# A two-layer graph kernel: the first batch's scores computed from h transposed, with the small weight products placed after the second row of scores

## The chip, the cores and the metric

The kernel runs on one core of a Trainium2 chip. The metric is device time in microseconds (us) of one execution; times shown are medians of several executions.

The core's engines work side by side, each through its own queue in order: TensorE (PE; PEld is its weight load), VectorE (DVE), ScalarE (ACT), GpSimd (POOL) and SyncE (SP), which only issues transfers. Transfers are also issued by ScalarE and GpSimd. An instruction waits on semaphores until its inputs are written and its output's buffer is free, and everything behind it in its queue waits too. Matrix products go to PSUM; the kernel's other tiles lie in SBUF.

## What is computed

There are 16 batches of 1024 nodes with 128 features, and an adjacency matrix of 1024 x 1024 for each. Layer 0, cut to what matters here:

```python
h = jnp.einsum('bnf,df->bnd', x, Ww) + Wb
e = jnp.einsum('bjl,bkl->bjk', jnp.einsum('bjd,dl->bjl', h, A), h)
e = e + jnp.swapaxes(e, 1, 2)
scores = jnp.where(adj > 0, e, 0.0)
attention = jax.nn.softmax(scores, axis=1) * adj
h_prime = jax.nn.relu(jnp.einsum('bij,bjk->bik', attention, h))
```

Three gates follow, of the kind `sigmoid(h_prime @ wi_u + x @ wi_x)`, then a tanh, a residual sum and a layer norm. Layer 1 has four heads, each with scores, a tanh of adjacency times scores and a product with its own projection. Its heads are averaged, added to the input, and normalized again.

With S = A + A^T, the symmetric scores are e = h S h^T. Since h = x Ww^T + Wb, the same scores can be had from x directly: a matrix Q = Ww^T S Ww, a column c = Ww^T S Wb and a per-row constant replace h.

## The kernel before

**Tiling.** A batch's 1024 nodes are 8 blocks of 128. `R` (P x 8 x 8 x 128) holds the scores of one batch; `R[:, :, j, :]` is row block j. Since the scores are symmetric, `score(j)` computes only the blocks from the diagonal on (in halves of 512 columns), and `turn_score(j)` makes the mirrored blocks: in batch 0 by TensorE transposes and a ScalarE copy, later by VectorE and transfers. `find_edges(j)` (L391) makes the 0/1 mask from the adjacency, `mask(j)` (L401) multiplies it in and takes the row maximum on VectorE, then takes the exponential on ScalarE. `weigh(j)` (L414) takes the reciprocal of the sum, scales h's block into `hz`, multiplies the row by the adjacency, and `back(j - 1)` (L431) accumulates the block before it into `acc`.

**Scores of all batches before the change.** `project_q` (L306) computes q^T = Q^T x^T + c, `score` multiplies a block of q^T with x^T, and ScalarE adds the row constant while it copies the product out (L353). That constant is the last column of `h`, which `multiply_h` and `add_h` (L323, L333) compute with width G = 132: 128 columns of h, three columns of x's gate products, and this constant. Hence the first batch's score copies need `h`, and `h` needs `wwT_g` with its gate columns and `wb_row` with its last column.

**The weights.** The top of the kernel loads A, Ww and the small vectors, then forms `a_sym` = A + A^T, `wwT`, `s_ww` = S Ww, `q_w` = Q and `c_col`, one after the other (L139 to L153). `weigh_bias` (L155) adds the three gate columns and S Wb, `finish_weights` (L161) the last constant. Between them `keep_at_work` has TensorE multiply zeros. `join_weights` (L166) prepares layer 1's weights in four parts; its first part is a subtraction on GpSimd (L169).

**Order.** The order of work is written by hand (`manual_schedule`). `run(first, "...")` issues the named pieces of batch 0: Qn is `project_q`, Hn and hn are `multiply_h` and `add_h` for groups of three blocks, En `find_edges`, Sn `score`, Tn `turn_score`, An `mask`, Bn `weigh`; "S1.0" is one half of row 1. Every engine's queue follows that order. Before, batch 0's order is:

```python
run(first, "Q0")
weigh_bias()
run(first, "H0")
finish_weights()
run(first, "h0 E0 E1 S0 T0.0 S1.0 T0.1 S1.1 A0 E2 Q1 T1 S2 A1 E3 H1 h1 B0 T2 S3 A2 E4 B1")
```

From batch 0's end on, a loop over 16 x 32 steps runs layer 1 of one batch with layer 0 of the next.

**Buffers.** All products of this part come from one PSUM pool of four buffers (`small` and the scores, tag "sc"), handed out in turn: a product waits for whoever reads the one four before. Transfers issued from SP and ScalarE share eight semaphores, handed out in program order, and so a transfer waits for the eighth before it: the adjacency loads (L300) wait for the small loads ahead of them.

Of the kernel before, what the change touches and what calls it, by code (L numbers as in the profile page):

```python
# [19 lines left out]
P = 128  # L20
# [4 lines left out]
def two_layer_adjacency_kernel(  # L25
# [29 lines left out]
    sb = ctx.enter_context(tc.tile_pool(name="sb", bufs=2))  # L55
# [5 lines left out]
    def small(name):  # L61
        return ps_sc.tile([P, 512], F32, tag="sc", name=name)
# [4 lines left out]
    ident = consts.tile([P, P], F32, name="ident")  # L67
# [2 lines left out]
    nc.gpsimd.memset(mhalf, -0.5)  # L70

    a_in = sb.tile([P, P], F32, tag="hz", name="a_in", bufs=4)
    nc.scalar.dma_start(a_in, A)
    ww_in = sb.tile([P, P], F32, tag="hz", name="ww_in", bufs=4)
    nc.sync.dma_start(ww_in, Ww)
    wb_col = consts.tile([P, 1], F32, name="wb_col")
    nc.scalar.dma_start(wb_col, Wb.rearrange("(d o) -> d o", o=1))
    rows_x = sb.tile([3, P], F32, tag="s1", name="rows_x", bufs=4)
    for g, w in enumerate((wi_x, wf_x, wo_x)):
        nc.scalar.dma_start(rows_x[g : g + 1], w.rearrange("(o d) -> o d", o=1))  # L80


    G = D + 4
# [4 lines left out]
    wwT = wwT_g[:, :D]  # L88
# [46 lines left out]
    def keep_at_work(n):  # L135
        for _ in range(n):
            nc.tensor.matmul(idle[:, :P], warm[:, :P], warm[:, :P], start=True, stop=True)  # L137

    keep_at_work(6)  # L139
    pa, pw, ps, pc = small("p_a"), small("p_ww"), small("p_s"), small("p_c")  # L140
    nc.tensor.transpose(pa[:, :P], a_in, ident)
    nc.vector.tensor_add(a_sym, pa[:, :P], a_in)
    nc.tensor.matmul(pw[:, :P], ww_in, ident, start=True, stop=True)
    nc.scalar.copy(wwT, pw[:, :P])
    nc.gpsimd.tensor_copy(b_wide, wb_col.to_broadcast([P, P]))
    nc.tensor.matmul(ps[:, :P], a_sym, ww_in, start=True, stop=True)
    nc.vector.tensor_copy(s_ww, ps[:, :P])
    keep_at_work(1)
    pq, px = small("p_q"), small("p_x")
    nc.tensor.matmul(pq[:, :P], s_ww, ww_in, start=True, stop=True)  # L150
    nc.vector.tensor_copy(q_w, pq[:, :P])
    nc.tensor.matmul(pc[:, 0:1], s_ww, wb_col, start=True, stop=True)
    nc.vector.tensor_copy(c_col, pc[:, 0:1])  # L153

    def weigh_bias():  # L155
        nc.tensor.matmul(px[:, :3], rows_x, ident[:3, :3], start=True, stop=True)
        nc.vector.tensor_copy(gate_x, px[:, :3])
        nc.tensor.matmul(px[:, 3:4], a_sym, wb_col, start=True, stop=True)
        nc.vector.tensor_copy(sb_col, px[:, 3:4])

    def finish_weights():  # L161
        pt = small("p_bsb")
        nc.tensor.matmul(pt[:, :1], b_wide, sb_col, start=True, stop=True)
        nc.vector.tensor_copy(wb_row[:, G - 1 : G], pt[:, :1])
# [118 lines left out]
    def layer0(b):  # L283
# [5 lines left out]
        t = {}  # L289
# [16 lines left out]
        def project_q(q):  # L306
            if q == 0:
                t["qT"] = sb.tile([P, N], F32, tag="qT0", name=f"qT0_{b}", bufs=1)
            if (b, q) == (0, 1):
                ps = small("pT_q0_second")  # L310
                nc.tensor.matmul(ps, q_w, t["xT"][:, 512:], start=True, stop=True)
                nc.vector.tensor_scalar_add(t["qT"][:, 512:], ps, c_col)
                return
            if (b, q) != (0, 0):
                return project_T(t["qT"], q_w, t["xT"], c_col, f"q0_{b}", [q])
            ps = small("pT_q0_first")
            nc.tensor.matmul(ps, q_w, t["xT"][:, :512], start=True, stop=True)
            for at, to in ((0, P), (P, 512)):
                nc.scalar.activation(
                    t["qT"][:, at:to], ps[:, at:to], AF.Identity, bias=c_col  # L320
                )

        def multiply_h(g):  # L323

# [18 lines left out]
        def score(j, halves=None):  # L343
            if j == 0 and "R" not in t:

                t["R"] = sb.tile([P, NB, NB, P], F32, tag="R", name=f"R_{b}", bufs=1)
            for q in range(j // BH, NH) if halves is None else halves:
                ps = ps_sc.tile([P, 512], F32, tag="sc", name=f"sc0_{b}_{j}_{q}")
                lo, at = max(q * 512, j * P), (q + 1) * 512
                nc.tensor.matmul(  # L350
                    ps[:, : at - lo], t["qT"][:, ts(j, P)], t["xT"][:, lo:at], start=True, stop=True
                )
# [45 lines left out]
            engine.tensor_scalar(m, adj_t[b, j], 0.0, None, ALU.is_gt)  # L398
            t["edge", j] = m.rearrange("p (k d) -> p k d", d=P)

        def mask(j):  # L401
            s, nmax = t["R"][:, :, j, :], -3e38
            for ks in (ts(0, BH), ts(1, BH)) if (b, j) == (0, 0) else [slice(NB)]:
                top = sb.tile([P, 1], F32, tag="top", name=f"top_{b}_{j}_{ks.start}", bufs=4)
                nc.vector.tensor_tensor_reduce(  # L405
                    s[:, ks], s[:, ks], t["edge", j][:, ks], 1.0, nmax, ALU.mult, ALU.max, top
                )
                nmax = top
            nmax = sb.tile([P, 1], F32, tag="nmax", name=f"nmax_{b}_{j}", bufs=4)
            nc.vector.tensor_scalar_mul(nmax, top, -1.0)  # L410
            t["z", j] = sb.tile([P, 1], F32, tag="z", name=f"z_{b}_{j}", bufs=4)
            nc.scalar.activation(s, s, AF.Exp, bias=nmax, accum_out=t["z", j])  # L412

        def weigh(j):  # L414

            s = t["R"][:, :, j, :]
            adj = adj_t[b, j].rearrange("p (k d) -> p k d", d=P)
            rz = sb.tile([P, 1], F32, tag="rz", name=f"rz_{b}_{j}", bufs=4)
            t["hz", j] = sb.tile([P, D], F32, tag="hz", name=f"hz_{b}_{j}", bufs=4)
            nc.vector.reciprocal(rz, t["z", j])  # L420
            if b == 0 and j in (0, 1, NB - 3, NB - 2, NB - 1):
                nc.vector.tensor_scalar_mul(t["hz", j], t["h"][:, j, :D], rz)
            else:
                nc.scalar.mul(t["hz", j], t["h"][:, j, :D], rz)

            for ks in (ts(0, BH), ts(1, BH)) if (b, j) == (0, NB - 1) else [slice(NB)]:
                nc.vector.tensor_mul(s[:, ks], s[:, ks], adj[:, ks])  # L427
            if j:
                back(j - 1)
# [110 lines left out]
        def finish(p):  # L540
# [5 lines left out]
        pieces = {  # L546
            "W": load_xT, "X": load_x, "R": relu,
        }
# [15 lines left out]
        for q in range(NH):  # L564
            pieces[f"Q{q}"] = partial(project_q, q)
# [5 lines left out]
            if j + 1 < NB:  # L571
                pieces[f"T{j}"] = partial(turn_score, j)
        if b == 0:
            del pieces["S1"], pieces["T0"]
        if b == 1:
            del pieces["S0"]
            for q in range(NH):
                pieces[f"S0.{q}"] = partial(score, 0, [q])
        return pieces

    def run(pieces, names):
        for name in names.split():
            if name in pieces:
                pieces.pop(name)()
# [144 lines left out]
    first, second, join = layer0(0), layer0(1), join_weights()  # L729
# [2 lines left out]
    run(first, "X")  # L732
    run(second, "W")
    run(second, "L0 L1 L2 L3 L4 L5 L6 L7")
    run(first, "Q0")
    weigh_bias()
    run(first, "H0")
    finish_weights()
    run(first, "h0 E0 E1 S0 T0.0 S1.0 T0.1 S1.1 A0 E2 Q1 T1 S2 A1 E3 H1 h1 B0 T2 S3 A2 E4 B1")
    next(join)  # L740
    run(first, "H2 h2 T3 S4 A3 E5")
    next(join)
# [1 line left out]
    next(join)  # L744
    run(first, "B3 T5 S6 A5 E7")
    next(join, None)
    run(first, "B4 T6 S7 A6")
    run(second, "Q0")
    run(first, "B5 A7")
    run(second, "H0")  # L750
    run(first, "B6 B7 R")
    run(second, "h0 H1")
    run(first, "P")
    run(second, "h1")
# [131 lines left out]
```

## Time and profile before

| | |
|---|---|
| median of 3 runs | 2412.29 us (2412.1 to 2412.39) |
| profiled execution | 2412.01 us, of it a span of 2410.1 us |
| first scores start (TensorE) | 9.44 us |
| first half mask starts (VectorE) | 12.02 us |
| mask of row 1 starts | 15.48 us |
| mask of row 2 starts | 19.43 us |
| first product into `acc` | 19.56 us |
| last multiplication by adjacency ends | 41.1 us |
| batch 0's gates start (VectorE) | 46.43 us |

All entries below the second line are starts or ends in the profiled execution, counted from the span's start. In the views shown further on, a line gives start and length in us (or a group's busy time), the engine, the line of the program, the operation, output and inputs with their shape, and in brackets how long the engine had been idle and what ended that.

### The profile page before, as it was taken

How to read it: one execution, taken by the hardware profiler on the slowest of the kernel's cores; microseconds unless marked ns; L12 is line 12 of the kernel's file. 1: busy time of each engine (PE TensorE's matmuls, PEld its weight loads, DVE VectorE, ACT ScalarE, POOL GpSimd, SP SyncE). 2: the span in 40 equal slices, each digit the busy share in tenths (PEclk: the TensorE clock that was granted, in tenths of full speed). 3: DMA queues.
4: the chain of work that ended last, by engine and by line, in shares of the span. 5: the costliest groups of instructions: out<-in, count | busy, mean ns of one | idle time of the engine just before them, and what ended most of it. 6: DMA issues, size and time to landing. Idle time of an engine off the chain costs nothing.

```text
span 2410.1 us, 20163 instructions
## 1 busy us (share of the span) xinstructions
PE 2400.0 (100%) x5981; PEld 1095.2 (45%) x5981; DVE 1552.6 (64%) x3264; ACT 1062.2 (44%) x1499; POOL 609.1 (25%) x390
## 2 busy tenths in 40 slices
PE   9999999999999999999999999999999999999999
PEld 5444444444444444444444444444444444444444
DVE  7666666666667666676666665666666576666555
ACT  6544344444444444445344454434444344443333
POOL 1314131241312413123131231313214132141000
PEclk9999999999999999999999999999999999999999
DMA  5334151441514324143242422325233252341010
GB/s 186 79 76 126 37 139 35 95 115 48 127 44 100 101 54 122 51 108 86 61 114 58 114 73 70 105 61 122 62 77 107 52 127 57 80 114 34 18 27 10
DMA packets 474370, 197.05 MB, mean 82 GB/s; under 512 B 414980, under 2 KB 440323, under 8 KB 474260
## 3 DMA queue, kind: packets, MB, share of 16 engines
q1 hardware_dynamic: 455645, 129.03, 22.8%
q0 software_dynamic: 18320, 66.66, 9.3%
q8 instruction: 48, 0.79, 0.1%
q14 instruction: 63, 0.51, 0.1%
q10 hardware_dynamic: 294, 0.07, 0.0%
HBM read 136.19 MB, written 59.51 MB: 81 GB/s over the span
## 4 chain that ended last, share of the span: by engine, by line
PE 98%; DVE 2%; ACT 0%; issue 0%; POOLq 0%; DVEq 0%; ACTq 0%
PE sc L634 36%; PE acc L640 36%; PE acc L435 9%; PE sc L350 5%; PE pR L605 5%; PE pT_u L234 5%; PE pR_h L331 1%; PE pT_q L234 1%; DVE R L405 0%; DVE R L427 0%; PE idle L137 0%; DVE s L635 0%; DVE st L210 0%; DVE edge L398 0%; PE pt L454 0%
## 5 line engine op out<-in xcount | busy, mean ns | idle before, releaser
L635 DVE TENSOR_TENSOR s<-sc,adj 128x512 f32<-128x512 f32 x1008 | 685.2, 688 | 714.7 <-PE sc L634 693.5
L636 ACT ACTIVATE s<-s 128x1024 f32<-128x1024 f32 x504 | 533.0, 1058 | 1057.0 <-DVE s L635 893.5
L634 PE MATMUL sc<-uT,x1T 128*128 128x512 f32 x2048 | 962.7, 592 | 0.2
L640 PE MATMUL acc<-s,h 128*128 128x512 f32 x2016 | 947.3, 592 | 0.0
L640 PEld LDWEIGHTS acc<-s,h 128*128 128x128 f32 x2016 | 380.5, 190 | 484.7 <-issue 477.5
L634 PEld LDWEIGHTS sc<-uT,x1T 128*128 128x128 f32 x2048 | 386.7, 190 | 470.2 <-issue 403.2
L398 POOL TENSOR_SCALAR edge<-adj 128x1024 uint8<-128x1024 f32 x120 | 332.6, 2772 | 316.2 <-DVE top_None L405 313.8
L214 POOL TENSOR_TENSOR rs<-rs,mhalf 128x8 f32<-128x8 f32 (+3 forms) x35 | 54.1, 1546 | 884.1 <-DVE rs L213 884.1
L435 PE MATMUL acc<-R,hz 128*128 128x512 f32 x512 | 240.7, 593 | 1.3 <-DVE R L427 1.2
L412 ACT ACTIVATE R<-R,nmax 128x1024 f32<-128x1024 f32 x128 | 147.0, 1148 | 86.2 <-DVE nmax L410 77.4
L405 DVE CUSTOM_DVE_ANT_0 R<-R,edge 128x1024 f32<-128x1024 f32 (+1 forms) x128 | 154.8, 1209 | 0.6 <-PE turn L385 0.4
L427 DVE TENSOR_TENSOR R<-R,adj 128x1024 f32<-128x1024 f32 x129 | 154.5, 1198 | 0.0
L435 PEld LDWEIGHTS acc<-R,hz 128*128 128x128 f32 x512 | 96.7, 190 | 122.3 <-issue 115.2
L350 PE MATMUL sc<-xT,qT 128*128 128x512 f32 (+3 forms) x384 | 145.1, 487 | 0.6 <-ACT R L353 0.6
L353 ACT ACTIVATE R<-sc,h 128x512 f32<-128x512 f32 (+1 forms) x192 | 110.6, 579 | 51.4 <-PE sc L350 46.2
L467 POOL TENSOR_TENSOR x1T<-hp,wu_b 128x1024 f32<-128x1024 f32 x45 | 106.4, 2364 | 103.0 <-DVE hws L473 63.7
L234 PE MATMUL pT_u<-x1T,ms 128*128 128x512 f32 x256 | 120.6, 592 | 0.2 <-ACT x1T L598 0.2
L605 PE MATMUL pR<-cw,x1T 128*128 128x512 f32 x256 | 117.6, 598 | 0.0
L350 PEld LDWEIGHTS sc<-xT,qT 128*128 128x128 f32 x384 | 69.5, 190 | 71.0 <-issue 60.0
L300 POOL DMA_DIRECT2D adj<-in_adjT_dram x112 | 65.7, 587 | 92.5 <-DVE s L635 92.5
L658 DVE SCALAR_TENSOR_TENSOR sum<-acc,sum 128x512 f32<-128x512 f32 x95 | 61.3, 687 | 42.2 <-PE acc L640 42.2
L608 ACT COPY h<-pR 128x512 f32<-128x512 f32 x128 | 72.3, 592 | 28.3 <-PE pR L605 26.6
(144 smaller groups left out, 1131.5 us busy)
## 6 DMA issues: line engine op xcount, KB each, us to landing
adj<-in_adjT_dram POOLq DMA_DIRECT2D x112, 512.0 KB, 4.0
adj<-in_adjT_dram SPq DMA_DIRECT2D x16, 512.0 KB, 8.7
x<-in_x_dram SPq DMA_DIRECT2D x16, 512.0 KB, 5.6
xT<-in_xT_dram SPq DMA_DIRECT2D x15, 512.0 KB
dram_hp<-turn_hp SPq DMA_DIRECT2D x15, 512.0 KB, 2.6
hp<-dram_hp SPq DMA_DIRECT2D x60, 128.0 KB, 3.1
dram_x<-turn_x SPq DMA_DIRECT2D x15, 512.0 KB, 3.0
x1T<-dram_x SPq DMA_DIRECT2D x60, 128.0 KB, 5.8
```

The source lines that it names most:

```text
L234: nc.tensor.matmul(ps, w, src[:, ts(q, 512)], start=True, stop=True)
L350: nc.tensor.matmul(ps[:, : at - lo], t["qT"][:, ts(j, P)], t["xT"][:, lo:at], start=True, stop=True)
L398: engine.tensor_scalar(m, adj_t[b, j], 0.0, None, ALU.is_gt)
L405: nc.vector.tensor_tensor_reduce(s[:, ks], s[:, ks], t["edge", j][:, ks], 1.0, nmax, ALU.mult, ALU.max, top)
L412: nc.scalar.activation(s, s, AF.Exp, bias=nmax, accum_out=t["z", j])
L427: nc.vector.tensor_mul(s[:, ks], s[:, ks], adj[:, ks])
L435: nc.tensor.matmul(t["acc"][:, ts(q, 512)], t["hz", j], t["R"][:, ts(q, BH), j, :], start=(j == 0), stop=(j == NB - 1),)
L605: nc.tensor.matmul(ps, x1T_t[b][:, ts(k, P)], cw.rearrange("p h d -> p (h d)"), start=True, stop=True)
L634: nc.tensor.matmul(ps, x1T[:, ts(m, P)], uT[:, ts(q, 512)], start=True, stop=True)
L635: nc.vector.tensor_mul(s[:, ts(q, 512)], ps, adj[:, ts(q, 512)])
L636: nc.scalar.activation(s, s, AF.Tanh)
L640: nc.tensor.matmul(acc[:, ts(q, 512)], h1[:, ts(hd, D)], s[:, ts(q, 512)], start=(m == 0), stop=(m == NB - 1),)
```

## The change

Batch 0 takes its scores from h^T and g = S h^T. h^T is projected in two halves (`project_h`, `place_h`), g in three parts of 128, 384 and 512 columns (`project_g`; the first copied out by VectorE, the others by ScalarE), and the scores' copies are plain copies without a bias. Later batches keep Q, c and the row constant.

The weights' order follows: Ww and Wb's column are loaded first on ScalarE's queue, A third, the three row vectors on GpSimd's queue. The products for Q, c, the gate columns and S Wb (`weigh_all`) are issued after row 1's scores, and so are H0, `finish_weights` and h0. The first mask is split into halves issued apart from each other, with its exponential as a piece of its own. The edges of rows 1 to 4 move later in VectorE's queue. `hz` of blocks 1 and 5 is scaled by ScalarE instead of VectorE. At the end of batch 0, batch 1's Q0 and H0 move behind B5 and B6.

```diff
     a_in = sb.tile([P, P], F32, tag="hz", name="a_in", bufs=4)
-    nc.scalar.dma_start(a_in, A)
     ww_in = sb.tile([P, P], F32, tag="hz", name="ww_in", bufs=4)
-    nc.sync.dma_start(ww_in, Ww)
+    nc.scalar.dma_start(ww_in, Ww)
     wb_col = consts.tile([P, 1], F32, name="wb_col")
     nc.scalar.dma_start(wb_col, Wb.rearrange("(d o) -> d o", o=1))
+    nc.scalar.dma_start(a_in, A)
     rows_x = sb.tile([3, P], F32, tag="s1", name="rows_x", bufs=4)
     for g, w in enumerate((wi_x, wf_x, wo_x)):
-        nc.scalar.dma_start(rows_x[g : g + 1], w.rearrange("(o d) -> o d", o=1))
+        nc.gpsimd.dma_start(rows_x[g : g + 1], w.rearrange("(o d) -> o d", o=1))
...
     keep_at_work(6)
-    pa, pw, ps, pc = small("p_a"), small("p_ww"), small("p_s"), small("p_c")
-    nc.tensor.transpose(pa[:, :P], a_in, ident)
-    nc.vector.tensor_add(a_sym, pa[:, :P], a_in)
-    nc.tensor.matmul(pw[:, :P], ww_in, ident, start=True, stop=True)
+    pa, pw = small("p_a"), small("p_ww")
+    nc.tensor.transpose(pw[:, :P], ww_in, ident)
     nc.scalar.copy(wwT, pw[:, :P])
...
+    def sum_A():
+        nc.tensor.matmul(pa[:, :P], a_in, ident, start=True, stop=True)
+        nc.vector.tensor_add(a_sym, pa[:, :P], a_in)
+        nc.gpsimd.tensor_copy(b_wide, wb_col.to_broadcast([P, P]))
+
+    def weigh_Ww():
+        ps = small("p_s")
+        nc.tensor.matmul(ps[:, :P], a_sym, ww_in, start=True, stop=True)
+        nc.vector.tensor_copy(s_ww, ps[:, :P])
+
+    def weigh_all():
+        pq, px = small("p_q"), small("p_x")
+        nc.tensor.matmul(pq[:, :P], s_ww, ww_in, start=True, stop=True)
+        nc.tensor.matmul(px[:, 4:5], s_ww, wb_col, start=True, stop=True)
         nc.tensor.matmul(px[:, :3], rows_x, ident[:3, :3], start=True, stop=True)
+        nc.tensor.matmul(px[:, 3:4], a_sym, wb_col, start=True, stop=True)
+        nc.vector.tensor_copy(q_w, pq[:, :P])
+        nc.vector.tensor_copy(c_col, px[:, 4:5])
         nc.vector.tensor_copy(gate_x, px[:, :3])
-        nc.tensor.matmul(px[:, 3:4], a_sym, wb_col, start=True, stop=True)
         nc.vector.tensor_copy(sb_col, px[:, 3:4])
...
+        def project_h(q):
+
+            if q == 0:
+                t["hT"] = sb.tile([P, N], F32, tag="turn", name="hT", bufs=2)
+            hT, at = t["hT"], q * 512
+            ps = small(f"p_hT_{q}")
+            nc.tensor.matmul(ps, wwT, t["xT"][:, ts(q, 512)], start=True, stop=True)
+            if q:
+                t["p_hT"] = ps
                 return
...
             for at, to in ((0, P), (P, 512)):
-                nc.scalar.activation(
-                    t["qT"][:, at:to], ps[:, at:to], AF.Identity, bias=c_col
-                )
+                nc.scalar.activation(hT[:, at:to], ps[:, at:to], AF.Identity, bias=wb_col)
+
+        def place_h():
+            nc.vector.tensor_scalar_add(t["hT"][:, 512:], t["p_hT"], wb_col)
+
+        def project_g(at, to):
+            if at == 0:
+                t["qT"] = sb.tile([P, N], F32, tag="qT0", name=f"qT0_{b}", bufs=1)
+            ps = small(f"p_g_{at}")[:, : to - at]
+            nc.tensor.matmul(ps, a_sym, t["hT"][:, at:to], start=True, stop=True)
+            (nc.scalar.copy if at else nc.vector.tensor_copy)(t["qT"][:, at:to], ps)
...
                 nc.tensor.matmul(
-                    ps[:, : at - lo], t["qT"][:, ts(j, P)], t["xT"][:, lo:at], start=True, stop=True
+                    ps[:, : at - lo], t["qT"][:, ts(j, P)], t["xT" if b else "hT"][:, lo:at],
+                    start=True, stop=True,
                 )
+                if b == 0:
+                    nc.scalar.copy(
+                        t["R"][:, lo // P : at // P, j, :],
+                        ps[:, : at - lo].rearrange("p (k d) -> p k d", d=P),
+                    )
+                    continue
...
-            if b == 0 and j in (0, 1, NB - 3, NB - 2, NB - 1):
+            if b == 0 and j in (0, NB - 2, NB - 1):
                 nc.vector.tensor_scalar_mul(t["hz", j], t["h"][:, j, :D], rz)
             else:
                 nc.scalar.mul(t["hz", j], t["h"][:, j, :D], rz)
...
-    run(first, "Q0")
-    weigh_bias()
+    run(first, "K0")
+    sum_A()
+    run(first, "K1 g0 k1")
+    weigh_Ww()
+    run(first, "S0.0 S0.1 E0 T0.0 A0.0 g1 T0.1 A0.1")
+    run(first, "S1.0 S1.1 A0.e E1")
+    weigh_all()
     run(first, "H0")
     finish_weights()
-    run(first, "h0 E0 E1 S0 T0.0 S1.0 T0.1 S1.1 A0 E2 Q1 T1 S2 A1 E3 H1 h1 B0 T2 S3 A2 E4 B1")
+    run(first, "h0 T1 S2 A1 E2 g2 H1 h1 B0 E3 T2 S3 A2 E4 B1")
...
-    run(first, "B4 T6 S7 A6")
+    run(first, "B4 T6 S7 A6 B5 A7")
     run(second, "Q0")
-    run(first, "B5 A7")
+    run(first, "B6")
     run(second, "H0")
-    run(first, "B6 B7 R")
+    run(first, "B7 R")
```

Kn is `project_h`, k1 `place_h`, gn `project_g`, "A0.0" and "A0.1" the halves of the first mask and "A0.e" its exponential.

More of the change, by code (lines that the diff above doesn't have):

```diff
@@ L139, in two_layer_adjacency_kernel @@
     keep_at_work(6)
-    pa, pw, ps, pc = small("p_a"), small("p_ww"), small("p_s"), small("p_c")
-    nc.tensor.transpose(pa[:, :P], a_in, ident)
-    nc.vector.tensor_add(a_sym, pa[:, :P], a_in)
-    nc.tensor.matmul(pw[:, :P], ww_in, ident, start=True, stop=True)
+    pa, pw = small("p_a"), small("p_ww")
+    nc.tensor.transpose(pw[:, :P], ww_in, ident)
     nc.scalar.copy(wwT, pw[:, :P])
-    nc.gpsimd.tensor_copy(b_wide, wb_col.to_broadcast([P, P]))
-    nc.tensor.matmul(ps[:, :P], a_sym, ww_in, start=True, stop=True)
-    nc.vector.tensor_copy(s_ww, ps[:, :P])
     keep_at_work(1)
[L149 to L155, printed above, removed]
+    def sum_A():
[10 more added lines that the diff above has]
+        nc.tensor.matmul(px[:, 4:5], s_ww, wb_col, start=True, stop=True)
         nc.tensor.matmul(px[:, :3], rows_x, ident[:3, :3], start=True, stop=True)
+        nc.tensor.matmul(px[:, 3:4], a_sym, wb_col, start=True, stop=True)
+        nc.vector.tensor_copy(q_w, pq[:, :P])
+        nc.vector.tensor_copy(c_col, px[:, 4:5])
         nc.vector.tensor_copy(gate_x, px[:, :3])
-        nc.tensor.matmul(px[:, 3:4], a_sym, wb_col, start=True, stop=True)
         nc.vector.tensor_copy(sb_col, px[:, 3:4])
@@ L308, in project_q @@
                 t["qT"] = sb.tile([P, N], F32, tag="qT0", name=f"qT0_{b}", bufs=1)
[L309 to L312, printed above, removed]
+            project_T(t["qT"], q_w, t["xT"], c_col, f"q0_{b}", [q])
+        def project_h(q):
[6 more added lines that the diff above has]
+                t["p_hT"] = ps
                 return
[L314 to L317, printed above, removed]
             for at, to in ((0, P), (P, 512)):
-                nc.scalar.activation(
-                    t["qT"][:, at:to], ps[:, at:to], AF.Identity, bias=c_col
-                )
+                nc.scalar.activation(hT[:, at:to], ps[:, at:to], AF.Identity, bias=wb_col)
[7 more added lines that the diff above has]
+            (nc.scalar.copy if at else nc.vector.tensor_copy)(t["qT"][:, at:to], ps)
         def multiply_h(g):
@@ L399, in find_edges, with mask, exponentials @@
             t["edge", j] = m.rearrange("p (k d) -> p k d", d=P)
[L401 to L404, printed above, removed]
+        def mask(j, halves=None):
+            s, nmax = t["R"][:, :, j, :], t.get("top", -3e38)
+            for ks in [slice(NB)] if halves is None else [ts(q, BH) for q in halves]:
+                t["top"] = sb.tile([P, 1], F32, tag="top", name=f"top_{b}_{j}_{ks}", bufs=4)
                 nc.vector.tensor_tensor_reduce(
-                    s[:, ks], s[:, ks], t["edge", j][:, ks], 1.0, nmax, ALU.mult, ALU.max, top
+                    s[:, ks], s[:, ks], t["edge", j][:, ks], 1.0, nmax, ALU.mult, ALU.max, t["top"]
                 )
-                nmax = top
-            nmax = sb.tile([P, 1], F32, tag="nmax", name=f"nmax_{b}_{j}", bufs=4)
-            nc.vector.tensor_scalar_mul(nmax, top, -1.0)
+            if halves != [0]:
+                t["nmax", j] = sb.tile([P, 1], F32, tag="nmax", name=f"nmax_{b}_{j}", bufs=4)
+                nc.vector.tensor_scalar_mul(t["nmax", j], t.pop("top"), -1.0)
+            if halves is None:
+                exponentials(j)
+        def exponentials(j):
+            s = t["R"][:, :, j, :]
             t["z", j] = sb.tile([P, 1], F32, tag="z", name=f"z_{b}_{j}", bufs=4)
-            nc.scalar.activation(s, s, AF.Exp, bias=nmax, accum_out=t["z", j])
+            nc.scalar.activation(s, s, AF.Exp, bias=t["nmax", j], accum_out=t["z", j])
         def weigh(j):
@@ L573, in layer0 @@
         if b == 0:
-            del pieces["S1"], pieces["T0"]
-        if b == 1:
+            del pieces["S1"], pieces["T0"], pieces["A0"], pieces["Q0"], pieces["Q1"]
+            for q in range(NH):
+                pieces[f"K{q}"] = partial(project_h, q)
+                pieces[f"A0.{q}"] = partial(mask, 0, [q])
+            for g, (at, to) in enumerate(((0, P), (P, 512), (512, N))):
+                pieces[f"g{g}"] = partial(project_g, at, to)
+            pieces["k1"] = place_h
+            pieces["A0.e"] = partial(exponentials, 0)
+        if b <= 1:
             del pieces["S0"]
```

## The prediction

> **What bounds the kernel now.** I read the page first, then the chain of waits over the first 24 us, then the order of time there.
>
> ```profile
> span 2410.1 us, 20163 instructions
> PE 2400.0 (100%) x5981; PEld 1095.2 (45%) x5981; DVE 1552.6 (64%) x3264; ACT 1062.2 (44%) x1499; POOL 609.1 (25%) x390
> ```
>
> TensorE is busy 2400.0 of 2410.1 us, so no more than some ten microseconds can be won at all. The change touches only batch 0's first layer, the first 45 us. There the chain (start, length, what) is TensorE's until the first scores, then VectorE's:
>
> ```profile
> 8.68 0.78 PE pR_h L331 x6
> 9.47 0.12 PE p_bsb L163 x2
> 9.58 1.82 PE sc L350 x4
> ...
> 14.72 0.68 DVE qT L312
> ...
> 15.48 1.23 DVE R L405
> ...
> 17.50 0.48 DVE h L335
> ...
> 18.29 1.22 DVE R L427
> 19.51 1.14 DVE R L405
> ...
> 21.55 0.94 DVE hz L422
> ...
> 22.58 1.21 DVE R L427
> ```
>
> From 15.48 on VectorE runs mask (L405), edges, multiplication (L427) back to back, until 41.1. A shift of these steps moves all later work: at 57 us TensorE starts a stretch that hardly stops again. In order of time (start, length, engine, line) two more things are seen:
>
> ```profile
> 9.62 0.16 DVE L164 COPY wb_row<-p_bsb 128x1 f32<-128x1 f32 x1 [0.74 <-PE p_bsb L163]
> 9.81 0.57 DVE L335 TENSOR_TENSOR h<-pR_h,wb_row 128x396 f32<-128x396 f32 x1
> 20.90 1.68 POOL L169 TENSOR_TENSOR cw<-cw_in,cw_last 128x512 f32<-128x512 f32 x1 [0.41 <-DMA cw_in<-in_L_gnn_conv_w_dram]
> 21.55 1.11 DVE L422 TENSOR_SCALAR hz<-h,rz 128x128 f32<-128x128 f32 x1
> ```
>
> The small weight products and h's first add are over at 10.4, before any mask. And hz for block 1 takes 1.11 us where its kind takes 0.29: it ends as GpSimd's subtraction ends (22.58).
>
> **What the Trainium skill says.** "SBUF — State Buffer", Who interferes with whom: VectorE and GpSimd share a port pair, held for a whole instruction; a VectorE instruction in a two-port mode, or with two SBUF inputs beside a GpSimd read, is blocked. The 1.11 us agrees. "TensorE: Matmul & The Clock Gate", Part 1: TensorE starts at half clock and warms after some 3.4 us of work, at a varying moment. Agrees: weight loads take 337 ns until 5.5 us and 190 ns from 5.74. "DMA: Bandwidth & Descriptors", Queues, rings and completion order: an engine serves the queues in turn, so a small transfer waits behind packets of others. Wb's column (0.5 KB) took 3.8 us to land, Ww (64 KB) 2.1.
>
> **The change part by part.** Prices from the trace: a score of 512 columns holds TensorE 0.86 (two passes of 0.43), one of 384 0.65, a 128-column pass 0.11; a result reaches the next engine 0.3 after the last pass. I walk each engine's queue in the changed order, starting each step when its engine and inputs are free.
>
> 1. Front. Ww comes first on ScalarE's queue (issue 0.72, lands at 2.85 as before), and its transpose takes A's place at 3.76, so wwT is there at 4.4. h^T's first half is projected from 4.4; at half clock until 5.6 it takes 1.5 instead of 0.86, result 6.2. ScalarE's 128 columns: 6.65. A's transpose and sum lie behind: a_sym 6.8. h^T's second half 6.2 to 7.0, g's first block 7.0, VectorE's copy 7.5 to 7.8. First score at 7.84, was 9.44: 1.6 sooner. Unknown: Wb's column now feeds h^T; landing at 4.96 as before it has 1.2 us to spare, and A behind it must land by 5.95. How far the adjacency packets, now issued sooner, hold these two up no row shows. Bounds: nothing, or 0.5 late and then a_sym 0.5 late; a warm clock at 4.6 instead of 5.6 makes all 0.5 sooner. I take the old landings and the old clock.
> 2. First mask. Scores, turns and g1 (384 columns, put between the turns) give halves of the mask at 10.35 and 11.43, nmax at 12.3, was 13.89: lead 1.6. ScalarE's plain copies save 0.11 each (L353's 0.69 against L386's 0.58). Edge 0 sits ahead at 8.6; its adjacency landed at 9.45 before, but its issue no longer waits (2.96 was A's landing; now about 1.6), so about 8.1. Even at 9.45 it would be done before 10.35.
> 3. Small products. g1's copy is done at 11.5, so row 1's scores hold TensorE 11.5 to 13.1. Only then come p_q and three thin products (0.22 each): 13.1 to 14.0. VectorE has run out (edge 1 ends 13.0): q_w 13.6; its three copies from p_x start behind one wait, 14.24. Then pR_h needs gate_x: 14.5 to 15.26, p_bsb, wb_row 15.74, h's add 15.93, mask 1 at 16.4. It was 15.48. Lead of 1.6 has become a loss of 0.9. Row vectors moved to GpSimd's queue are wanted at 13.5 and wb_row's broadcast, now behind them, at 15.9; that broadcast landed 6.4 after its issue at 1.6, so about 2 us later still clears.
> 4. g's last part. Row 2's scores wait for the PSUM buffer that h's add frees: 16.53. Then S2.1, g2 (0.86, new in this place) until 18.76, H1, and h1's add at 19.7, was 17.42. VectorE idles 1.2 us. First multiplication 20.57, was 18.29: 2.3 late.
> 5. Edges. Edge 2, done ahead of mask 1 before, now lies behind it, and edge 3 behind the multiplication: 0.6 more. Mask 2 at 22.3, was 19.43: 2.9 late.
> 6. Weighting on ScalarE. Block 1's hz leaves VectorE: from its reciprocal to the multiplication 22.58 - 21.36 = 1.22 becomes 0.07, so 1.15 won. Block 5's: 0.39 becomes 0.07, 0.3 won. ScalarE has gaps of 0.7 to 1.5 before each exponential there, which hide 0.40 each; without them the accumulation, not the mask, would wait. 2.9 - 1.15 - 0.3 = 1.4 late.
> 7. GpSimd's subtraction. Its inputs are sooner by about what the adjacency gains, 1.3 or a little more, so it runs near 19 to 20.2. VectorE's gap of step 4 (18.5 to 19.7) covers it, and h1's add reads PSUM. From 0 (hidden) to 1.1 (half of 1024 columns' 2.36 is 1.2; all of it blocks if it starts under a mask); I take 0.3.
>
> Row sums (S0.0/S0.1 split, the later Q0 and H0 of batch 1) move nothing: TensorE waits for VectorE there. h^T uses a buffer of the transposes' pool, free again long before batch 1's first turn. Later batches have the same instructions in the same order.
>
> Sum: 1.4 + 0.3 = +1.7 us. The profiled execution took 2412.01 (span 2410.1 and 1.9 around it), 0.28 under the median 2412.29; against the median this gives 2414.0. My walk, done for the old order, met the old trace within 0.3 us at every mask, so 0.5 either way is its own error.
>
> **The rivals.**
> - Other side, faster: the lead survives. Mechanism: the small products really hide behind row 1's scores, so that mask 1 starts when its turns allow. S1.1 copied at 14.0, six turns 0.8: mask 1 at 14.7, h1 no later than before plus 0.4. Then +0.4 + 0.6 - 1.45 = -0.5, or with a warm clock -1.0: 2411.5. It decides if mask 1 starts before 15.0. For: TensorE has gaps there. Against: h's add stands ahead of mask 1 in VectorE's queue, and needs four hand-overs after 13.1.
> - Worse: the port clash falls on a mask (0.8 more) and Wb's column or A lands late behind adjacency packets (0.5 more): 2415.3. For: three adjacency loads now start with no wait. Against: the gap of step 4.
> - No difference: the two roughly cancel, within 0.3 us of 2412.3. It takes the walk to be off by 1.4.
>
> **How the numbers follow.** Forecast 0.58, worse 0.20, faster 0.13, none 0.09. Forecast's own range, +0.8 to +2.6, is walk error and the clash's ends. Leaving out part of the two outer cases: 2411.3 to 2415.6. A change of 0.2%, about what a measurement of this kernel can tell from no change, is 4.8 us. Every case lies inside it; 0.05 of the chances above goes to something unseen that carries a case beyond it (a change in the repeated part, or a row vector from GpSimd's queue that lands very late): faster 0.02, same 0.95, slower 0.03.
>
> **What would show it.** First score near 7.8 and nmax 0 near 12.3 (steps 1, 2); mask 1 after 16, with VectorE idle before wb_row (3); h1's add near 19.7, released by TensorE (4); mask 2 near 22 (5); hz of block 1 on ScalarE and mul 1 near 24.4 (6); GpSimd's subtraction near 19 (7). Mask 1 before 15.0, or h1's add before 18, would prove me wrong; so would any change of time between 100 and 2400 us.

## The result

| | before | after |
|---|---|---|
| median, 16 executions each | 2412.24 us (2411.88 to 2415.8) | 2417.72 us (2415.17 to 2419.08) |
| ratio, 95% interval | | 1.002 (1.0013 to 1.0027) |
| profiled execution | 2412.01 us | 2417.81 us |

The changed kernel is slower by 5.5 us. The forecast was +1.7 us; the measured time lies above its range and above the "worse" rival. The page of the changed kernel:

```profile
span 2415.9 us, 20184 instructions
PE 2403.4 (99%) x5987; PEld 1097.1 (45%) x5987; DVE 1552.1 (64%) x3263; ACT 1062.8 (44%) x1503; POOL 610.7 (25%) x393
```

TensorE's busy time rose by 3.4 us, the other engines' by less than 2, the span by 5.8. So TensorE stands idle 2.4 us longer and is slower over part of its work, and both have to be looked for in the first 52 us, where batch 0's first layer ends. The chain of waits of the changed kernel (start, length, what) begins with a line that the old one did not have:

```profile
1.64 7.35 DMA a_in<-in_L_gnn_A_dram
8.98 0.04 issue
9.03 0.80 PE p_a L146 x2
9.82 1.71 PE p_hT L322 x2
11.53 0.43 PE p_g L336 x2
11.96 0.39 PE p_s L152 x2
12.35 0.08 issue
12.43 1.95 PE sc L366 x4
...
21.00 1.23 DVE R L428
...
26.52 1.13 DVE R L428
```

A's transfer, third on ScalarE's queue, is issued at 1.64 and takes 7.35 us. The forecast needed it by 5.95; it came at 9.0. The first score starts at 12.43 instead of 7.84 (it was 9.44 before the change). In order of time (start, length, engine, line, operation; in brackets the idle time and what ended it):

```profile
9.03 0.80 PE L146 MATMUL p_a<-ident,a_in 128*128 128x128 f32 x2 [2.86 <-DMA a_in<-in_L_gnn_A_dram]
...
9.62 1.91 PE L322 MATMUL p_hT<-xT,wwT_g 128*128 128x512 f32 x2
```

TensorE stood idle for 2.86 us, and then the second half of h^T took 1.91. The table by stretches of time shows why (its first line names the columns: the stretch, its length, the busy time and instructions of each engine, the granted TensorE clock, the DMA engines' share, GB/s):

```profile
core 0: us, PE busy (x) PEld busy (x) DVE busy (x) ACT busy (x) POOL busy (x), PEclk, DMA share, GB/s
6.00:7.00 1.00, 0.17 (x1) 0.00 (x0) 0.00 (x0) 0.79 (x2) 0.00 (x0) 1.00 0.91 355
7.00:8.00 1.00, 0.00 (x0) 0.00 (x0) 0.00 (x0) 0.05 (x1) 0.00 (x0) 1.00 1.48 395
8.00:9.00 1.00, 0.00 (x0) 0.00 (x0) 0.00 (x0) 0.00 (x0) 0.00 (x0) 0.89 0.77 204
9.00:10.00 1.00, 0.97 (x3) 0.93 (x4) 0.14 (x1) 0.00 (x0) 0.00 (x0) 0.50 0.97 324
```

While TensorE waits, the DMA engines move 355 and 395 GB/s, far more than the 64 KB of A. And the granted clock, 1.00 at 6, is 0.50 at 9. Stretches of half a microsecond give 0.78 for 8.5 to 9.0 and 0.81 for 12.0 to 12.5, which puts the half clock at about 8.8 to 12.2. (A reading of 1.00 in this column does not prove full clock: in the run "column as one row" below, the first half of h^T took 2.08 us at readings of 1.00. The reading of 0.50 is trusted here because the duration of the products goes with it.)

From the first score on, the changed kernel runs almost as the forecast walked it. The table gives times after the start of the first score; "loads of before" is the experiment further down in which A is on time.

| after the first score, us | forecast | after | loads of before |
|---|---|---|---|
| first score itself starts at | 7.84 | 12.43 | 7.41 |
| mask of row 1 | 8.6 | 8.57 | 8.57 |
| h1's add | 11.9 | 11.41 | 11.32 |
| mask of row 2 | 14.5 | 14.01 | 14.04 |
| second multiplication | 16.6 | 16.01 | 16.93 |

Batch 0's gates start on VectorE at 51.97 (46.43 before): 5.54 late, the whole loss.

```profile
51.97 0.18 DVE L529 TENSOR_TENSOR gate<-hp,gate 128x24 f32<-128x24 f32 x1 [1.90 <-ACT hp L483]
```

The first score is 2.99 later than in the kernel before, and 4.59 later than the forecast had it (12.43 against 7.84), because the lead of 1.6 is gone too. So the first question is what held A, and the second whether the rest of the sum would have come true with A on time.

### The profile page after: what moved, and what is told of

Same layout as the page of the kernel before. It is cut to its first block, busy times and chain, and to the rows that moved or that the text cites. A ratio compares the mean times of both kernels' runs of the same rounds, so it can differ in the third digit from the quotient of the medians.

```text
span 2415.9 us, 20184 instructions
## 1 busy us (share of the span) xinstructions
PE 2403.4 (99%) x5987; PEld 1097.1 (45%) x5987; DVE 1552.1 (64%) x3263; ACT 1062.8 (44%) x1503; POOL 610.7 (25%) x393
## 4 chain that ended last, share of the span: by engine, by line
PE 97%; DVE 1%; DMA 1%; issue 0%; ACT 0%; SPq 0%; POOL 0%; ACTq 0%; POOLq 0%; DVEq 0%
PE sc L669 36%; PE acc L675 36%; PE acc L463 9%; PE sc L366 5%; PE pT_u L239 4%; PE pR L640 4%; PE pR_h L347 1%; PE pT_q L239 1%; DMA a_in<-in_L_gnn_A_dram 0%; DVE R L428 0%; DVE st L215 0%; DMA R<-dram_turn 0%; SPq L269 0%; DVE x L230 0%; DVE R L455 0%
## 5 line engine op out<-in xcount | busy, mean ns | idle before, releaser
L366 PE MATMUL sc<-xT,qT 128*128 128x512 f32 (+2 forms) x360 | 135.7, 487 | 0.6 <-ACT R L376 0.6
L376 ACT ACTIVATE R<-sc,h 128x512 f32<-128x512 f32 (+2 forms) x180 | 103.8, 579 | 48.3 <-PE sc L366 43.2
```

The source lines that it names most:

```text
L366: nc.tensor.matmul(ps[:, : at - lo], t["qT"][:, ts(j, P)], t["xT" if b else "hT"][:, lo:at], start=True, stop=True,)
```

## The experiments

Each kernel was run beside the kernel before on the same chip. "Gates" is the start of batch 0's gates on VectorE in the profiled execution, against 46.43 before.

| kernel | A lands | column lands | first score | gates later by | time against before, us | ratio, 95% interval |
|---|---|---|---|---|---|---|
| after | 9.0 | 5.7 | 12.43 | 5.54 | +5.5 | 1.0013 to 1.0027 |
| A before the column | 4.7 | 8.0 | 9.53 | 2.81 | +3.0 | 1.0005 to 1.0018 |
| row vectors on ScalarE | 9.4 | 5.3 | 12.94 | 7.01 | +6.0 | 1.0013 to 1.0027 |
| TensorE kept at work | 9.0 | 5.6 | 10.98 | 4.04 | +4.4 | 1.0007 to 1.002 |
| column as one row | 8.4 | - | 11.87 | 5.21 | +5.2 | 1.0012 to 1.0026 |
| adjacency held | 4.9 | 4.6 | 8.77 | 2.88 | +2.8 (one execution) | - |
| A first on SP | 2.7 | 5.3 | 8.06 | 2.43 | +2.3 | 1.0 to 1.0017 |
| loads of before | in time | 4.5 | 7.41 | 1.42 | +1.7 | 0.9997 to 1.0013 |
| products sooner | in time | 4.8 | 8.07 | -0.52 | 0.0 | 0.9991 to 1.0007 |
| subtraction on TensorE | in time | 5.0 | 9.30 | 2.03 | +1.4 | 0.9992 to 1.0008 |
| hz 1 and 5 on ScalarE alone | as before | as before | as before | -0.79 | -0.65 | 0.9988 to 1.0005 |

Landings are the issue time plus the transfer's time to landing. The columns of the gates and of the time agree within about 1 us in every row, so the stretch up to the gates does decide the time. Where an interval includes 1, the time alone does not tell the kernel from the one before, and only the traces speak. Each trace is one execution. The last row is the kernel before with one edit, "products sooner" and "subtraction on TensorE" build on "loads of before", and the other rows are the changed kernel with one edit.

**A before the column.** Is it A's size or its place?

```diff
     nc.scalar.dma_start(ww_in, Ww)
+    nc.scalar.dma_start(a_in, A)
...
     nc.scalar.dma_start(wb_col, ...)
-    nc.scalar.dma_start(a_in, A)
```

> The changed kernel with one edit: on ScalarE's queue A is issued ahead of Wb's column instead of behind it. Theory (A waits behind the column's 128 four-byte packets and the adjacency packets): A lands before 5 us instead of 9.0, TensorE doesn't stop at 6.2 and its clock doesn't fall back to half, first score near 7.8 to 8.5 instead of 12.4, time 2413.2 to 2414.2, that is +1.0 to +2.0 over before: what the forecast's walk had. Rival (adjacency traffic alone holds A, wherever it stands in its queue): A still lands after 8, time stays within 1 of 2417.7. Second rival (the time is lost in the later order, steps 3 to 5): A lands early and the time stays above 2416.

A, now second, took 3.5 us to land. The column, now third, with 0.5 KB, took 6.4 and held h^T, so that the first score and the time came later than expected (9.53, and 3.0 above the kernel before). So the place decides, or the moment of issue: in these two runs 1.2 was early enough and 1.6 was not. Size does not.

**Row vectors on ScalarE.** They go behind A as before the change. Through the eight shared semaphores, this makes all adjacency loads but the first wait for earlier loads again.

```diff
-        nc.gpsimd.dma_start(rows_x[g : g + 1], ...)
+        nc.scalar.dma_start(rows_x[g : g + 1], ...)
```

> The changed kernel with one edit: the three row vectors go back to ScalarE's queue, behind A, so that seven of the eight adjacency loads wait for small loads again, as before. Theory that early adjacency traffic holds A: A lands near 6, time 2414 to 2415. Rival that A's place behind Wb's column alone holds it: A still lands near 9, time within 1 of 2417.7.

A landed 7.8 us after its issue all the same. This seemed to clear the adjacency, but one line of the adjacency's transfers in that run, up to 1.9 us, says otherwise:

```profile
L305 SPq DMA_DIRECT2D adj<-in_adjT_dram x1: 432/432/432, 1.6 to 1.6; - x1
```

One load of 512 KB was still issued at 1.6, beside A, and three more at 3.7, 5.2 and 5.6, before A had landed. So this run left the cause open between these loads and the place in the queue. It lost more than the changed kernel, 7.0 us at the gates, and two things in its trace have a part in that: the half clock was granted from 8.06 to about 14.9, 6.8 us instead of 3.4, although TensorE worked again from 9.5 on, and mask 1 ran beside GpSimd's subtraction and took 2.14 instead of 1.23.

**TensorE kept at work.** Thirteen products of zeros fill the wait for A. How much of the loss is the clock?

```diff
     run(first, "K0")
+    keep_at_work(13)
     sum_A()
```

> The changed kernel plus 13 products of zeros on TensorE between h^T's first half and A's product, 2.8 us of work where it stood still. A still lands near 9. If the half clock from 8.9 to 12.2 us was a cost of its own: first score about 1 us sooner (11.4 instead of 12.4), time about 2416.7. If it cost nothing: within 0.3 of the changed kernel's own 2417.7.

A still landed at 9.0, but the second half of h^T took 1.02 instead of 1.91 and the first score started 1.45 us sooner:

```profile
9.35 1.02 PE L322 MATMUL p_hT<-xT,wwT_g 128*128 128x512 f32 x2
```

The half clock is worth 1.5 us at the gates (5.54 - 4.04). In the time it is 1.1 (5.5 - 4.4), a difference that the intervals alone would not show. The rest of A's lateness, against the forecast's first score, is 10.98 - 7.84 = 3.14.

**Adjacency held.** The adjacency loads are not issued until A is there.

```diff
         def load_adj(j):
...
+            if (b, j) == (0, 0):
+                nc.gpsimd.tensor_copy(a[:, :1], a_in[:, :1])
             (nc.sync if b < 2 else nc.gpsimd).dma_start(a, adjT[b, ts(j, P), :])
```

> The changed kernel, but the adjacency loads are not issued until A has landed: a GpSimd copy of one column of A into the first adjacency tile goes ahead of them. Theory 1 (adjacency packets, issued sooner than before, hold A up): A lands at 4.5 to 6. Theory 2 (its third place on ScalarE's queue, behind the column, holds it up, together with x^T's half-megabyte at most): A lands at 7.5 or later all the same. First adjacency row then lands 4 to 6 us after A, so the first edges and all later masks are later than in the changed kernel under theory 2.

The two answers of the trace for A's transfer, first of the changed kernel, then of this one. The second line of each gives the time from issue to landing:

```profile
L77 ACTq DMA_DIRECT2D a_in<-in_L_gnn_A_dram x1: 453/453/453, 1.6 to 1.6; - x1
...
DMA to landing us min/median/max: 7.3/7.3/7.3
```

```profile
L77 ACTq DMA_DIRECT2D a_in<-in_L_gnn_A_dram x1: 454/454/454, 1.6 to 1.6; - x1
...
DMA to landing us min/median/max: 3.2/3.2/3.2
```

Same queue, same place behind the column, same moment of issue: 7.3 against 3.2. The adjacency loads held A, for 4.1 us. What is ahead of A, the column and x^T, can account for no more than part of the 3.2. The row vectors gained too (2.5 to 3.5 us to landing instead of 6.3 to 7.3). Keeping the adjacency back cost nothing at the first edge, which ran at 9.39 without waiting for it. The first score, 8.77, would have come sooner still with the clock of the other runs: h^T's first half took 2.08 here and 1.40 in the changed kernel. This is one execution, but the 7.3 stands in two traces, of the changed kernel and of the one kept at work.

**Column as one row.** It comes as 512 bytes that TensorE turns, instead of 128 pieces of 4 bytes.

```diff
-    nc.scalar.dma_start(wb_col, Wb.rearrange("(d o) -> d o", o=1))
+    wb_in = sb.tile([1, P], F32, tag="s1", name="wb_in", bufs=4)
+    nc.scalar.dma_start(wb_in, Wb.rearrange("(o d) -> o d", o=1))
...
+    nc.tensor.matmul(pw[:, P : P + 1], wb_in, ident[:1, :1], start=True, stop=True)
+    nc.vector.tensor_copy(wb_col, pw[:, P : P + 1])
```

> The changed kernel, but Wb's column comes as one row of 512 bytes that TensorE turns, instead of 128 pieces of 4 bytes. Theory 2a (the column's 128 small packets hold A up): A lands at 4.5 to 5.5, the first score at 7.8 to 8.5, time 1.5 to 2.5 us above the kernel before. Theory 2b (third place holds it up whatever is ahead) or theory 1 (adjacency): A lands at 8 or later, first score after 11.5, time 4 us or more above.

A took 6.7 us, landing at 8.4, so the column's small packets account for about 0.6 of its 7.3 us. The packets in this trace show how A was held: between 3.6 and 5.5 us ScalarE's queue moved 0.06 MB in 126 packets, nearly all of A; the last few packets, 18 at most, took until 8.4, while SP's queue moved 0.84 MB between 5.5 and 8.5. The load counts as landed with its last packet.

**A first on SP.**

```diff
-    nc.scalar.dma_start(a_in, A)
+    nc.sync.dma_start(a_in, A)
```

> The changed kernel with one transfer moved: A goes first on SP's queue, ahead of x^T and the adjacency, and no longer third on ScalarE's. Theory (A was late because adjacency packets were issued ahead of it or beside it): A lands at 2.8 to 3.5, the column at 5 to 6, the first score at 7.8 to 8.8, mask 1 at 16.3 to 17.4, time 1.5 to 2.8 us above the kernel before. Rival (the column, too, is held up by the sooner adjacency and takes A's place as the last to land): column after 7, first score after 9.5, time 3 or more above.

```profile
L77 SPq DMA_DIRECT2D a_in<-in_L_gnn_A_dram x1: 382/382/382, 0.7 to 0.7; - x1
...
DMA to landing us min/median/max: 2.0/2.0/2.0
```

A landed 2.0 us after its issue, the column 4.1 after its own. One moved transfer takes 3.1 of the gates' 5.5 us away, while the adjacency is still issued right behind x^T, at 2.1 instead of 1.6.

**Loads of before.** The changed order of work, with the small loads on the queues and in the order that they had.

> The changed order of work, but all small loads as before: A first and Wb's column second on ScalarE's queue, the row vectors behind them, Ww first on SP. Theory (late A is what the forecast missed; its other steps hold): A lands near 2.9, the column near 5.0, TensorE does not idle and keeps its clock; first score 7.8 to 8.2, mask 1 16.2 to 16.8, h1's add 19.4 to 20.1, mask 2 22.0 to 22.7; time 1.2 to 2.2 us above the kernel before. Rival a (the later steps were mis-sized too and cost more than walked): 3 us or more above. Rival b (with the loads right the lead survives): no more than 0.3 above.

The median is 1.7 us above that of the kernel before (2413.92 against 2412.21). The interval still includes no change, so the trace has to carry this reading: the gates are 1.42 late. In order of time, the steps that the forecast named, with GpSimd's subtraction:

```profile
15.98 1.23 DVE L428 CUSTOM_DVE_ANT_0 R<-R,edge 128x1024 f32<-128x1024 f32 x1
...
18.73 0.57 DVE L351 TENSOR_TENSOR h<-pR_h,wb_row 128x396 f32<-128x396 f32 x1 [0.73 <-PE pR_h L347]
...
21.45 1.21 DVE L428 CUSTOM_DVE_ANT_0 R<-R,edge 128x1024 f32<-128x1024 f32 x1
...
22.77 1.57 DVE L421 TENSOR_SCALAR edge<-adj 128x1024 bf16<-128x1024 f32 x1
```

```profile
21.50 2.30 POOL L174 TENSOR_TENSOR cw<-cw_in,cw_last 128x512 f32<-128x512 f32 x1 [0.51 <-DMA cw_in<-in_L_gnn_conv_w_dram]
```

Mask 1 comes 15.98 - 15.48 = 0.5 later than in the kernel before although the first score is 2.0 sooner: the lead is lost in the small products, as step 3 said. An edge that takes 0.68 elsewhere takes 1.57 and ends at 24.34, after the subtraction's end at 23.80. The subtraction was blocked in its turn: it began at 21.50, beside the mask that ran from 21.45 to 22.66, and ended 1.14 after that mask.

**hz of blocks 1 and 5 on ScalarE alone**, in the kernel before.

```diff
-            if b == 0 and j in (0, 1, NB - 3, NB - 2, NB - 1):
+            if b == 0 and j in (0, NB - 2, NB - 1):
```

> The kernel before with one edit: hz of blocks 1 and 5 is scaled by ScalarE (step 6 alone). Forecast's working: VectorE saves 1.15 + 0.3, so 1.0 to 1.5 faster than before, 2410.8 to 2411.3, unless GpSimd's subtraction then blocks another VectorE instruction (edge 4 or the next mask) by up to 1.1; then 0 to 0.4 faster. Rival: the accumulation waits for ScalarE instead and nothing is won (within 0.2 of 2412.2).

The median is 0.65 us lower, with an interval that includes no change, and between the two amounts that the expectation had named; in the trace the gates come 0.79 sooner. The second multiplication started 1.2 sooner, at 21.39; but then GpSimd's subtraction met the next mask, which took 1.95 instead of 1.21:

```profile
22.14 1.58 POOL L169 TENSOR_TENSOR cw<-cw_in,cw_last 128x512 f32<-128x512 f32 x1 [0.28 <-DMA cw_in<-in_L_gnn_conv_w_dram]
```

```profile
22.86 1.95 DVE L405 CUSTOM_DVE_ANT_0 R<-R,edge 128x1024 f32<-128x1024 f32 x1
```

**Products sooner.** On top of the loads of before, the order that the steps 3 to 5 charge is mended.

```diff
     run(first, "S0.0 S0.1 E0 T0.0 A0.0 g1 T0.1 A0.1")
-    run(first, "S1.0 S1.1 A0.e E1")
     weigh_all()
-    run(first, "H0")
+    run(first, "S1.0 S1.1 A0.e E1 E2 H0")
     finish_weights()
-    run(first, "h0 T1 S2 A1 E2 g2 H1 h1 B0 E3 T2 S3 A2 E4 B1")
+    run(first, "h0 T1 S2 A1 E3 H1 h1 g2 B0 T2 S3 A2 E4 B1")
```

> As the version with all loads of before, and further: the small weight products are issued ahead of row 1's scores instead of behind them, edge 2 ahead of h's first add, edge 3 ahead of h's second, and g's last part behind H1. Theory (steps 3 to 5 of the forecast are losses of the order and not of the formula): mask 1 at 15.0 to 15.7, h1's add at 17.5 to 18.2, mask 2 at 19.5 to 20.3; time 0.2 to 1.5 us below the kernel before. Rival (small products now delay row 1's scores and turns by as much as they gain): mask 1 after 16, time 0.5 to 1.5 above the kernel before.

```profile
15.70 1.23 DVE L428 CUSTOM_DVE_ANT_0 R<-R,edge 128x1024 f32<-128x1024 f32 x1
...
19.64 1.22 DVE L428 CUSTOM_DVE_ANT_0 R<-R,edge 128x1024 f32<-128x1024 f32 x1
...
23.11 1.95 DVE L428 CUSTOM_DVE_ANT_0 R<-R,edge 128x1024 f32<-128x1024 f32 x1
```

The masks came as expected, the gain in time did not: the time is that of the kernel before (2412.2 against 2412.21), the gates are 0.5 sooner in the trace. Counted from the first score (8.07), mask 1 starts at 7.63 instead of 8.57, mask 2 at 11.57 instead of 14.04. So of the losses in steps 3 to 5, 2.5 us belong to the order and not to the formula. Of what was won by mask 2, 0.7 goes again at mask 3, which took 1.95 beside the subtraction. The first score itself was 0.66 later than with the loads of before, although nothing ahead of it was changed; h^T's first half took 1.53 us, and 1.12 with the loads of before. By so much can two traces of the same front differ.

**Subtraction on TensorE.** To see what the version without that clash would bring. The edit is cut to the subtraction itself; the parts of `join_weights` also come one step later in the order, and `cw_last` is loaded as one row.

```diff
-        nc.gpsimd.memset(cw_last[0:1], 0.0)
-        nc.gpsimd.tensor_sub(cw, cw_in, cw_last)
+        pt = small("p_cw")
+        nc.tensor.matmul(pt, ident, cw_in.rearrange("p h d -> p (h d)"), start=True, stop=False)
+        nc.tensor.matmul(pt, minus, cw_last.rearrange("p h d -> p (h d)"), start=False, stop=True)
+        nc.scalar.copy(cw.rearrange("p h d -> p (h d)"), pt)
```

> As the version with the products sooner, but cw = cw_in - cw_last is formed by TensorE (identity times cw_in, and a row of -1 times the last row, summed in PSUM; ScalarE copies it out), one step later in the order, so that GpSimd subtracts nothing; cw_last is loaded as one row of 2 KB instead of 128 copies. Theory (what is left of the loss is the shared port under mask 3, 1.95 instead of 1.22): mask 3 takes 1.25 at most, all later masks 0.7 sooner than there, time 0.6 to 1.6 us below the kernel before. Rival (TensorE's four extra passes and ScalarE's copy delay row 4's turns or h's last part): a wait of 0.5 or more ahead of mask 4, no gain.

Mask 3 took 1.22, but the next mask waited:

```profile
29.30 1.23 DVE L433 CUSTOM_DVE_ANT_0 R<-R,edge 128x1024 f32<-128x1024 f32 x1 [1.74 <-PE turn L396]
```

TensorE had no room for the four passes there: they stood from 24.84 to 26.91, ahead of the accumulation and of the turn that mask 4 waited for. The rival came true, and this profile's first score was late as well (9.30: h^T's first half took 1.91, and TensorE waited 0.47 for x^T's second half). No version was shown to beat the kernel before.

## Why the prediction was wrong

- **Step 1 failed**, in one term: "I take the old landings and the old clock", with 0.5 us as the upper bound. A landed at 9.0 instead of the 5.95 that the walk could bear, and TensorE, idle meanwhile, fell to half clock: 3.14 and 1.45 us at the first score. The mechanism had been named ("How far the adjacency packets hold these two up no row shows"), and its cause too (the adjacency issue "no longer waits"). Only its size had no ground: the 0.5 was not worked out from any row. The trace of before offered one, and step 3 even quotes it for another purpose: `wb_row`'s broadcast, 64 KB like A and issued at 1.6 like A, though on GpSimd's queue, took 6.4 us to land. With that, A would have been put at 8.0. The passage of the Trainium skill ("DMA: Bandwidth & Descriptors", Queues, rings and completion order) on queues served in turn agrees with the runs in kind: A's last packets trickled through while SP's queue moved its own. How long a small transfer is held it does not say, and here that was 4.1 us.
- **The rest of step 1.** Ww's old landing failed too, by 1.0 us (3.1 instead of 2.1), but that is not the adjacency's doing, since it took 3.2 with the adjacency held as well; with x^T issued at the same moment it took 3.1 to 3.2, with x^T issued 0.44 later 2.0 to 2.2. It cost little: h^T's first half started at 4.77 and not at 4.4. Otherwise the front held: in the run with the loads of before the first score came at 7.41, 0.4 sooner than walked, with the clock warm sooner (h^T's first half took 1.12 and not 1.5).
- **The clock** is what "TensorE: Matmul & The Clock Gate", Part 1 describes, from the other side: it was quoted for warming and not for what a wait brings. The page has the array return to half clock after an idle window of some 3.4 us. Measured, it came sooner: 2.6 us after the last product in the changed kernel, and 1.2 us after it in the run with the row vectors on ScalarE, where TensorE had also stood for 0.94 us just before that product. It stayed for 3.4 us (8.8 to 12.2) in the one and 6.8 us (8.1 to 14.9) in the other. For this kernel the measured waits decide, and a wait well under 3.4 us is already a risk.
- **Step 2** held in the changed kernel: 4.34 us from the first score to nmax 0 against 4.46 walked.
- **Step 3** held exactly: mask 1 8.57 after the first score, walked 8.56. Ordering the products ahead of row 1's scores brought it to 7.63.
- **Steps 4 and 5** were 0.4 to 0.5 too dear by h1's add and mask 2, no more; VectorE's wait ahead of h1 was 0.73 and not 1.2 in the run with the loads of before.
- **Step 6** had the size right (the second multiplication gains 1.2 in the kernel before) and what follows wrong: 1.45 walked, 0.65 measured alone (with an interval that includes no change), since the subtraction then meets the next mask.
- **Step 7** had the place wrong: the subtraction started at 21.48 in the changed kernel, not near 19. Its data is the last of a long line of loads on SP's queue, which did not finish sooner. In the changed kernel it blocked edge 2 (1.57 instead of 0.68), most of it inside the wait ahead of h1. With the loads of before it blocked edge 3, at 0.9 us, where 0.3 had been taken and 1.1 was the bound. As "SBUF — State Buffer", Who interferes with whom, says, the port is held for a whole instruction, and the traces show it both ways. Blocked edges ended 0.5 to 0.6 us after the subtraction and blocked masks 1.1, about as if they had started at its end (hz of block 1 in the kernel before ended only 0.08 after it). The subtraction waits in its turn: in the nine traces in which it began beside a mask, an edge or a multiplication of VectorE, it ended 1.11 to 1.14 us after that one; in two others it took 1.27. So the 1.2 us walked for it were right, and the recorded 1.58 to 2.30 shown here include its own wait.

At the gates the loss against the kernel before is 5.54. Against the walk, the first score is 4.59 late: 3.14 (A) + 1.45 (clock). What is left, 5.54 - 4.59 = 0.95, is what the rest of the walk came to, where the forecast had 1.7. The same order of work with the loads where they had been was 1.42 late at the gates and 1.7 in the median. So the later steps together were priced about right, and the moved loads, whose lateness was priced at nothing, cost the rest. That the median repeats the forecast's 1.7 is in part luck: the first score was 0.4 sooner than walked and steps 4 and 5 were 0.4 to 0.5 cheaper, while the clash cost 0.9 instead of 0.3, and the interval around that median includes no change. The faster rival fell with step 3: even with A in time mask 1 started at 15.98, not before 15.0. The worse rival named the first cause, A behind the adjacency, and gave it 0.5; the half clock it did not name, and its other half, a clash under a mask (0.8), did not come in the changed kernel.

What stays open is how the adjacency loads hold A's last packets for so long. Full DMA engines are not the whole answer: in the run with the row vectors on ScalarE they moved only 17 GB/s between 6.5 and 7.0, and A still landed at 9.4. Nor is it known whether the one load issued at 1.6 would do: that run had three more under way before A landed, and no run varied the number or size of these loads.

## What to carry to other kernels

When an edit lets a large load start sooner, price the small loads that are issued at the same moment or behind it, on every queue; the old landing of a small transfer holds only as long as what flows beside it is the same. A wait that seems to hold up a large load for nothing may be what lets the small ones through: look at what lands last ahead of the first dependent product, and issue that first. When a saving moves a chain on an engine by about a microsecond, look at what it will then meet on a port that it shares, as VectorE and GpSimd did here.

## What the runs showed of the hardware

- A transfer of 64 KB on ScalarE's queue, issued at 1.6 with adjacency loads of 512 KB issued from 1.6 on from SP's, took 6.7 to 7.8 us to land, one of 0.5 KB in that place 6.4. With the adjacency kept back until 5.07 the same 64 KB took 3.2 us, and issued ahead of everything on SP's queue 2.0. Ww, as large and first on its queue, took 3.1 to 3.2 beside x^T's load (issued at 0.72 as well) and 2.0 to 2.2 where x^T's was issued at 1.16.
- A late load was paid twice: in the changed kernel 2.86 us of idle TensorE brought the granted clock down to 0.50 until about 12.2, another 1.45 us at the first score. In the run with the row vectors on ScalarE a wait of 2.64 us brought it down until about 14.9.
- VectorE and GpSimd blocked each other for whole instructions: beside the subtraction an edge of 0.68 us took 1.57 and more and a mask of 1.21 took 1.95 and more, and the subtraction, 1.27 us where nothing blocked it, took up to 2.30.
- The times of the kernel before fall in two groups: in the comparison at the top fourteen executions at 2411.9 to 2412.4 us and two at 2415.6 and 2415.8. Those of the changed kernel spread from 2415.2 to 2419.1, those of the version kept at work from 2415.63 to 2416.98. What makes either spread, and whether the clock's moment has a part in it, was not tried.
